# A dilated unfold in one round of matmuls, its outer taps moved by SyncE's DMAs, and the store moved behind the next strip's

## The chip, the cores and the metric

The kernel runs on one core of a Trainium2 chip. The metric is the device time of one execution in microseconds; the median of three runs is given. Engines are named as in the profile: PE multiplies matrices, DVE is the vector engine, ACT the scalar engine, POOL is GpSimd, and SP is SyncE, which here only issues DMAs. Each engine works through its own instructions in order; engines meet at semaphores.

## The reference, cut to what matters

The input `x` is 2 x 128 x 256 x 256, in fp32 throughout. Two residual layers follow each other. Layer 0 normalises in groups, runs a windowed attention with a halo, and adds the result to `x`. Layer 1, the only one that the change touches, is this:

```python
def _L1_conv_ref(x, w1, w3, w4):
    ...
    t1 = jax.lax.conv_general_dilated(x, w1, window_strides=(1, 1), padding=((2, 2), (0, 0)))
    t3 = jax.lax.conv_general_dilated(t1, w3, window_strides=(1, 1), padding=((1, 1), (0, 0)), feature_group_count=c)
    t2 = _unfold_w3_dil2(x)
    t4 = jnp.einsum('nckhw,ckg->nghw', t2, w4[:, :, 0, :])
    t5 = t4[:, None, :, :, :] * t3.reshape(n, c // g, g, h, w)
    return t5.reshape(n, c, h, w)
...
x = x + _L1_conv_ref(_gn(x), L1_conv_w1, L1_conv_w3, L1_conv_w4)
```

`t1` is a vertical convolution of five taps over all 128 channels, and `t3` a vertical convolution of three taps for each channel by itself. `t4` is the horizontal part: `t2` holds, for every pixel, the values two columns to the left, at the pixel, and two columns to the right (zeros outside the image), and `t4` is their product with three 128 x 8 matrices, summed. The eight maps of `t4` are then multiplied into the 128 channels of `t3`, channel c using map c mod 8, and the input of the layer is added.

## The kernel before, in words

The attention layer comes first and writes its result to DRAM strip by strip (`x1_d`). The convolution layer, `convolutions_fast`, then runs over 64 strips: 2 images of 32 strips, 8 image rows each. Channels lie on the 128 partitions. The order of instructions on each engine is the order in which the loop writes them down (`manual_schedule` for all five engines). For strip k the loop does this:

- `load_rows1` (L636, L638) issues on SP the two loads of strip k+2 into one of six `raw` buffers.
- `unfold` (L692) makes `t4`. The 8 rows of the strip are four pairs j; pair j gets the 32 output partitions from 32j on, of which 8 are used. For each of the three taps there are four matmuls, one for each pair, reading the normalised rows `xm` at a column offset of 2 x tap and adding up in one PSUM bank `g`. ACT then copies the bank to `t4` in SBUF (L698).
- `first_rows` copies the two last rows of the strip before on ACT (L723).
- `start_strip` normalises strip k+1: ACT copies four rows that both strips share (L649), DVE normalises the eight new ones from `raw` (L651).
- `vertical(k, 2)` and later `vertical(k, 4)` make four rows of `t1` each, by a scheme that shares products between neighbouring rows: PE makes `a_c` (L706), `a_d` (L740), `a_e` and `a_o` (L706) in a ring of three PSUM banks; ACT copies `a_c` to `both` (L737); DVE makes `c` from `a_d` and `both` (L744) and adds it to `a_e` (L751) and to `a_o` (L757); ACT scales the four rows for the first tap of `t3` (L762).
- `row_sums(k + 1)` makes the next strip's row sums and differences, `sm` (L678 on DVE, one row by ACT, L677) and `df` (L682). It stands between the two halves.
- `depthwise` adds the other two taps of `t3` on DVE (L769, two instructions of 1024 elements per half).
- `spread` (L780) widens `t4` to 128 channels: four matmuls, one for each row pair, with the 0/1 matrix `sel`, of which each uses 32 partitions; the results stand in four banks `b`.
- `combine` (L789) multiplies each bank with its rows of `t3` into `y`, on DVE.
- `finish` (L797, L798) has POOL issue a DMA that adds `x1_d` onto `y`, and SP the store of `y`. SP waits for the first before it issues the second. The last strip is finished in halves with vector additions.

So SP's order is: loads of k+2, store of k, loads of k+3, store of k+1, and so on. `t4`, `t3` and `y` have two buffers each. In strips 1 to 7 some small instructions of the last image's normalisation and of a range test stand between.

Of the kernel before, what the change touches and what calls it, by code (L numbers as in the profile page):

```python
# [9 lines left out]
F32 = mybir.dt.float32  # L10
# [9 lines left out]
P = 128  # L20
W = 256
# [24 lines left out]

def host_constants():
    ident = np.eye(P, dtype=np.float32)  # L50
    gavg = np.zeros((P, P), np.float32)
    for g in range(P // 4):
        gavg[4 * g : 4 * g + 4, 4 * g : 4 * g + 4] = 0.25

    kb = np.zeros((HEADS, 32, 6, 10), np.float32)
    for c in range(10):
        kb[:, c, :, c] = 1.0
    for r in range(6):
        kb[:, 10 + r, r, :] = 1.0
    kb[:, 16, :, 6:] = NEG  # L60
    kb[:, 17, :, :4] = NEG
    flag = np.zeros((2, 4 * NPAIR * 4, 2, 4), np.float32)
    flag[0, :, 0] = 1.0
    flag[1, :, 1] = 1.0


    hot = np.zeros((2, HEADS, 16, 2, 64), np.float32)
    for key in range(64):
        j, i = divmod(key, 6)
        for e in range(2):  # L70
            if 0 <= j - 4 * e < 6:
                hot[:, :, j - 4 * e, e, key] = 1.0
            else:
                hot[:, :, 12, e, key] = NEG
            if key < 60:
                hot[:, :, 6 + i, e, key] = 1.0


    keep = np.zeros((2, HEADS, 16, 2, 2), np.float32)
    for i in range(2):  # L80
        keep[:, i::2, 0:12, i, 0] = 1.0
        keep[:, i::2, 12, i, 1] = 1.0

    sel = np.zeros((4, 32, P), np.float32)
    for ch in range(P):
        sel[:, ch % 8, ch] = 1.0
    return {
        "c_ident": ident,
        "c_sel": sel.reshape(P, P),
        "c_gavg": gavg,  # L90
        "c_kb": kb.reshape(P, 60),
        "c_flag": flag.reshape(2, 4 * NPAIR, 32),
        "c_hot": hot.reshape(P, 128),
        "c_keep": keep.reshape(P, 4),
        "c_head": np.stack([(np.arange(P) // DH % 2 == i) for i in range(2)], 1).astype(np.float32),
    }


class Norms:


    def __init__(self, nc, glob, small, gavg, ns):
        self.nc, self.glob, self.small, self.gavg, self.ns = nc, glob, small, gavg, ns
        self.done = {}
# [478 lines left out]
class Weights:  # L583


    def __init__(self, nc, io, glob):
        self.nc, self.io = nc, io
        self.w1 = glob.tile([P, 5, P], F32, tag="w1", name="w1")
        self.w3 = glob.tile([P, 3], F32, tag="w3", name="w3")
        self.w4 = glob.tile([P, 3, 32], F32, tag="w4", name="w4")  # L590
        self.sel = glob.tile([P, P], F32, tag="sel", name="sel")
        self.w1s = glob.tile([P, 6, P], F32, tag="w1s", name="w1s")

# [13 lines left out]
def convolutions_fast(tc, io, x1_d, norm, st_y, out, weights, count_good):  # L607

    nc = tc.nc
    NB, _, H, _ = io["x"].shape  # L610
    NS = H // 8
    with ExitStack() as l1:
        cst = l1.enter_context(tc.tile_pool(name="f_l1c", bufs=1))
        rawp = l1.enter_context(tc.tile_pool(name="f_raw1", bufs=6))
        tp = l1.enter_context(tc.tile_pool(name="f_t1", bufs=2))
        wk = l1.enter_context(tc.tile_pool(name="f_wk1", bufs=2))
# [4 lines left out]
        w1, w3, w4, sel, w1s = weights.w1, weights.w3, weights.w4, weights.sel, weights.w1s  # L621
# [7 lines left out]
        def load_rows1(b, s):  # L629

            if s == 0:
                pre = rawp.tile([P, 8, W], F32, tag="raw", name=f"raw1_{b}_pre")
                nc.sync.dma_start(pre[:, 5:8, :], x1_d[b][0][:, 0:3, :])
                raws[b, -1] = pre
            t = rawp.tile([P, 8, W], F32, tag="raw", name=f"raw1_{b}_{s}")
            nc.sync.dma_start(t[:, 0:5, :], x1_d[b][s][:, 3:8, :])  # L636
            if s + 1 < NS:
                nc.sync.dma_start(t[:, 5:8, :], x1_d[b][s + 1][:, 0:3, :])  # L638
            raws[b, s] = t
# [15 lines left out]
                nc.gpsimd.memset(cur[:, 4 + n : 12, :], 0.0)  # L655

        t1s, sms, dfs = {}, {}, {}

# [25 lines left out]
        def unfold(k):  # L686

            xt = xn[k % 2]
            pg = ps_pj.tile([P, 512], F32, tag="pj", name=f"g_{k}")
            for tap in range(3):  # L690
                for j in range(4):
                    nc.tensor.matmul(  # L692
                        pg[32 * j : 32 * j + 32, :], w4[:, tap, :],
                        xt[:, 2 * j + 1 : 2 * j + 3, 2 * tap : 2 * tap + W],
                        start=tap == 0, stop=tap == 2,
                    )
            t4 = wk.tile([P, 512], F32, tag="t4", name=f"t4_{k}")
            nc.scalar.copy(t4, pg)  # L698
            t3 = wk.tile([P, 8, W], F32, tag="t3", name=f"t3_{k}")
            y = wk.tile([P, 8, W], F32, tag="y", name=f"y_{k}")  # L700
            ts[k] = t4, t3, y
# [72 lines left out]
        def spread(k):  # L774

            t4 = ts[k][0]
            banks = []
            for j in range(4):
                pb = ps_b.tile([P, 512], F32, tag=f"b{j}", name=f"b_{k}_{j}")
                nc.tensor.matmul(  # L780
                    pb, sel[32 * j : 32 * j + 32, :], t4[32 * j : 32 * j + 32, :], start=True, stop=True
                )
                banks.append(pb)
            return banks
# [9 lines left out]
        def finish(k):  # L794
            b, s = divmod(k, NS)
            t4, t3, y = ts.pop(k)
            nc.gpsimd.dma_start(y, x1_d[b][s], accum_op=ALU.add)  # L797
            nc.sync.dma_start(out[b, :, 8 * s : 8 * s + 8, :], y)  # L798
            del raws[b, s - 1]

        def finish_half(k, half):

            b, s = divmod(k, NS)
            t4, t3, y = ts[k]
            if half == 0:
                nc.gpsimd.tensor_tensor(y[:, 0:3, :], y[:, 0:3, :], raws[b, s - 1][:, 5:8, :], ALU.add)
                nc.gpsimd.tensor_tensor(y[:, 3:4, :], y[:, 3:4, :], raws[b, s][:, 0:1, :], ALU.add)
            else:
                nc.vector.tensor_tensor(y[:, 4:8, :], y[:, 4:8, :], raws[b, s][:, 1:5, :], ALU.add)
            nc.sync.dma_start(  # L810
                out[b, :, 8 * s + 4 * half : 8 * s + 4 * half + 4, :], y[:, 4 * half : 4 * half + 4]
            )

        with tc.manual_schedule(engines=ORDERED):
            for k in range(2):
                load_rows1(*divmod(k, NS))
            start_strip(0)
            row_sums(0)
            for k in range(NB * NS):
                more = k + 1 < NB * NS  # L820
                if k + 2 < NB * NS:
                    load_rows1(*divmod(k + 2, NS))
                unfold(k)
                first_rows(k)
                if more:
                    start_strip(k + 1)

                vertical(k, 2)


                if k in (1, 2):
                    count_good[k - 1](ps_b, "b3")
                if k == 2:
                    steps = norm.steps(st_y[NB - 1], ps_b, f"y{NB - 1}", "b3")
                for _ in range({3: 1, 4: 2, 5: 2, 6: 1, 7: 1}.get(k, 0)):
                    next(steps)
                if more:
                    row_sums(k + 1)
                depthwise(k, 2)
                vertical(k, 4)  # L840
                banks = spread(k)
                combine(k, banks, (0, 1))
                if not more:
                    finish_half(k, 0)
                depthwise(k, 4)
                combine(k, banks, (2, 3))
                if more:
                    finish(k)
                else:
                    finish_half(k, 1)  # L850
# [559 lines left out]
def lay_out(inputs):  # L1410

    c = np.ascontiguousarray
    w_qkv = np.asarray(inputs["L0_conv_W_qkv"])
    rel = np.concatenate(
        [np.asarray(inputs["L0_conv_rel_width"]).T, np.asarray(inputs["L0_conv_rel_height"]).T], axis=1
    )
    w4 = np.asarray(inputs["L1_conv_w4"])[:, :, 0, :]
    return {
        "x": c(np.asarray(inputs["x"])),
        "w_qkvT": c(w_qkv.T),  # L1420
        "w_q": c(w_qkv[:P]),
        "w_outT": c(np.asarray(inputs["L0_conv_W_out"]).T),
        "relT": c(np.tile(rel, (HEADS, 1))),
        "w1T": c(np.asarray(inputs["L1_conv_w1"])[:, :, :, 0].transpose(1, 2, 0)),
        "w3": c(np.asarray(inputs["L1_conv_w3"])[:, 0, :, 0]),
        "w4": c(np.tile(w4, (1, 1, P // w4.shape[-1]))),
        "w4g": c(np.pad(w4, ((0, 0), (0, 0), (0, 32 - w4.shape[-1])))),
        **host_constants(),
    }

# [16 lines left out]
```

## Time and profile before

| what | value |
|---|---|
| median of three runs | 3217.13 us (3214.41 to 3219.65) |
| the profiled execution | 3215.36 us |
| its span | 3213.6 us |
| granted TensorE clock | 0.996 |
| attention, up to the first `unfold` at 2104 us: PE, DVE busy | 1991 us, 1639 us |
| convolutions, 2104 us to the end (1109.6 us): PE, DVE, ACT busy | 1090 us, 972 us, 331 us |

How it is read: all times of the trace are counted from the start of the span, in microseconds, and come from the one profiled execution. "Busy" is the time in which an engine has an instruction under way. A group is written as line, engine, operation, what is written and read, and the shape; `x1408` is the number of records, followed by the busy time in us, the mean ns of one, and the idle time just before its instructions with what ended it. A `SPq` row is the time that SP takes to issue a DMA. The stage of the attention is untouched by the change. The 40 slices show that the convolutions begin after slice 26:

```profile
PE   0799999999999999999999999989999999999998
DVE  8788888888888777777777777679888898888887
DMA  9433333333332222222222222146777676777775
```

### The profile page before, as it was taken

The page shows a single profiled execution, that of the slowest core. Times are in us where ns is not written, and L with a number is a line of the kernel's source. Part 1 is how long each engine was busy: PE and PEld are TensorE (multiplying, and loading weights), DVE is VectorE, ACT ScalarE, POOL GpSimd, SP SyncE. Part 2 cuts the span into 40 slices and gives each one's busy share as a digit, 9 for nine tenths or more (in the row PEclk, how much of TensorE's full clock was granted, in tenths as well). Part 3 has the DMA queues.
Part 4 walks back from the last instruction along what each step waited for, and adds up shares of the span by engine and source line. Part 5 has one row for each costly group of instructions (what it writes and reads, how often), then busy time and mean ns, then how long its engine had stood idle before and what let it go on. Part 6 is the DMA issues. An engine that isn't in the chain of part 4 may idle for free.

```text
span 3213.6 us, 117425 instructions
## 1 busy us (share of the span) xinstructions
PE 3081.7 (96%) x53030; PEld 2280.1 (71%) x53030; DVE 2611.1 (81%) x4152; ACT 1439.9 (45%) x2481; POOL 584.8 (18%) x917
## 2 busy tenths in 40 slices
PE   0799999999999999999999999989999999999998
PEld 0688998899998889999889998844444444444443
DVE  8788888888888777777777777679888898888887
ACT  0455555555555555555555555522332333233322
POOL 2222222222222222222222222100000000000001
PEclk9999999999999999999999999999999999999999
DMA  9433333333332222222222222146777676777775
GB/s 396 149 132 112 122 109 111 108 118 121 111 111 92 85 69 92 81 72 85 69 92 81 72 85 69 56 130 170 190 190 189 180 189 190 184 183 187 193 184 153
DMA packets 125116, 426.42 MB, mean 133 GB/s; under 512 B 9024, under 2 KB 75328, under 8 KB 92096
## 3 DMA queue, kind: packets, MB, share of 16 engines
q1 hardware_dynamic: 115536, 352.76, 32.2%
q0 software_dynamic: 9072, 66.06, 11.3%
q8 instruction: 420, 6.88, 0.9%
q14 instruction: 88, 0.72, 0.1%
HBM read 284.57 MB, written 134.22 MB: 130 GB/s over the span
## 4 chain that ended last, share of the span: by engine, by line
PE 85%; issue 10%; DVE 2%; DMA 1%; POOL 1%; ACT 0%; SPq 0%; POOLq 0%; DVEq 0%; ACTq 0%
PE f_pv L416 15%; PE f_pq L341 8%; PE f_s L451 8%; PE f_o L476 8%; PE a_e L706 7%; PE a_o L706 7%; PE f_pk L341 7%; PE f_py L341 7%; PE f_pa L395 4%; PE f_s L435 4%; PE g L692 4%; PE a_d L740 3%; PE b L780 2%; PE a_c L706 1%; DMA raw<-f_x 1%
## 5 line engine op out<-in xcount | busy, mean ns | idle before, releaser
L422 DVE COPY f_vt<-f_pv 64x512 f32<-64x512 f32 x512 | 354.4, 694 | 292.2 <-ACT f_vt L422 292.0
L416 PE MATMUL f_pv<-f_wqkvT,f_xn 128*128 128x128 f32 x4096 | 491.3, 278 | 0.0
L416 PEld LDWEIGHTS f_pv<-f_wqkvT,f_xn 128*128 128x128 f32 x4096 | 466.9, 192 | 8.6
L762 ACT ACTIVATE t<-t,w 128x1024 f32<-128x1024 f32 x128 | 147.3, 1151 | 687.2 <-DVE t L757 666.8
L323 POOL COPY f_xq<-f_xn 128x256 f32<-128x256 f32 x512 | 310.6, 651 | 756.1 <-DVE f_xn L309 756.1
L376 ACT ACTIVATE f_q<-f_pq,f_head 128x512 f32<-128x512 f32 x512 | 310.2, 688 | 303.4 <-PE f_pq L341 303.4
L460 ACT ACTIVATE f_p<-f_s 128x512 f32<-128x512 f32 x512 | 264.3, 602 | 404.2 <-PE f_s L451 404.2
L422 ACT COPY f_vt<-f_pv 64x512 f32<-64x512 f32 x512 | 297.3, 582 | 118.1 <-PE f_pv L416 117.9
L769 DVE SCALAR_TENSOR_TENSOR t<-t,w,t 128x1024 f32<-128x1024 f32 x256 | 329.9, 1289 | 7.6 <-ACT t L762 1.3
L451 PEld LDWEIGHTS f_s<-f_q,f_kt 64*64 64x64 f32 x16384 | 250.6, 135 | 49.2 <-issue 49.2
L341 PE MATMUL f_pq<-f_xn,f_wq_s 128*128 128x192 f32 (+2 forms) x1520 | 277.1, 329 | 3.3 <-DVE f_xn L309 2.5
L451 PE MATMUL f_s<-f_q,f_kt 64*64 64x64 f32 x16384 | 268.1, 220 | 0.0
L476 PE MATMUL f_o<-f_vt,f_p 128*32 128x66 f32 x16384 | 264.4, 222 | 1.1 <-issue 0.4
L797 POOL DMA_DIRECT2D y<-f_x x63 | 68.1, 1082 | 1017.5 <-DVE y L789 1003.5
L476 PEld LDWEIGHTS f_o<-f_vt,f_p 128*32 128x32 f32 x16384 | 242.5, 110 | 10.6 <-DVE f_cf L408 1.0
L341 PE MATMUL f_pk<-f_xn,f_wqkvT 128*128 128x256 f32 x1024 | 245.2, 380 | 0.0
L341 PEld LDWEIGHTS f_pq<-f_xn,f_wq_s 128*128 128x128 f32 x1520 | 232.4, 188 | 16.9 <-issue 4.2
L341 PE MATMUL f_py<-f_ot,f_woT 128*128 128x256 f32 x1024 | 241.7, 378 | 2.3 <-DVE f_ot L494 2.3
L706 PE MATMUL a_o<-xm,w1s 128*128 128x512 f32 x512 | 240.5, 590 | 0.5 <-ACT both L737 0.5
L706 PE MATMUL a_e<-xm,w1s 128*128 128x512 f32 x512 | 240.7, 591 | 0.0
L300 POOL COPY f_xn<-f_xn 128x1280 f32<-128x1280 f32 x62 | 86.9, 1402 | 772.0 <-PE f_pv L416 772.0
L510 DVE TENSOR_TENSOR f_x<-f_py,f_raw 128x512 f32<-128x512 f32 x256 | 176.0, 688 | 58.1 <-PE f_py L341 50.3
(126 smaller groups left out, 4607.7 us busy)
## 6 DMA issues: line engine op xcount, KB each, us to landing
f_raw<-in_x SPq DMA_DIRECT2D x62, 1280.0 KB, 7.8
f_sx<-in_x SPq DMA_DIRECT2D x64, 1024.0 KB, 7.2
f_x<-f_x SPq DMA_DIRECT2D x128, 512.0 KB, 3.3
y<-f_x POOLq DMA_DIRECT2D x63, 1024.0 KB, 8.2
out<-y SPq DMA_DIRECT2D x63, 1024.0 KB, 4.9
raw<-f_x SPq DMA_DIRECT2D x64, 640.0 KB, 6.4
raw<-f_x SPq DMA_DIRECT2D x62, 384.0 KB, 6.9
f_raw<-in_x SPq DMA_DIRECT2D x2, 1024.0 KB, 7.1
```

Of the source, the lines that this page charges most:

```text
L323: nc.gpsimd.tensor_copy(xq[:, t2, half].rearrange("p t r n c e -> p r t (n c) e"), cells[:, :, 16 * half : 16 * half + 16, 1 + t2 : 9 : 4, ...
L341: nc.tensor.matmul(dst[:, 32 * lo : 32 * hi], w, moving[:, lo:hi], start=True, stop=True)
L376: nc.scalar.activation(q[:, c, :, i], pq.rearrange("p (n x) -> p n x", n=NPAIR), AF.Copy, scale=head[:, i : i + 1],)
L416: nc.tensor.matmul(pv[:, P * n : P * n + P], xn[k % 2][:, r, 4 * j + n].rearrange("p c x -> p (c x)"), wvT, start=True, stop=True,)
L422: (nc.vector.tensor_copy if c else nc.scalar.copy)(vt[rows, 4 * j : 4 * j + 4, :, c, 0:32], pv[rows].rearrange("p (n h d) -> p n h d", n=4 ...
L451: nc.tensor.matmul(sc[g][n // 8][64 * c : 64 * c + 64, n % 8].rearrange("p i x -> p (i x)"), keys_k[rows, c, 48 * n : 48 * n + 64], qs[u][ ...
L460: nc.scalar.activation(pts[u][:, g, 8 * half : 8 * half + 8].rearrange("p n i x -> p (n i x)"), sc[g][half].rearrange("p n i x -> p (n i x ...
L476: nc.tensor.matmul(po[32 * h : 32 * h + 32, n - lo], p[:, h // 2, n, h % 2], vt[:, n, h], start=True, stop=True,)
L510: nc.vector.tensor_tensor(x1[:, :, c:W:2], py.rearrange("p (m t) -> p t m", t=4), raws[k][:, r:8:2, c:W:2], ALU.add,)
L706: nc.tensor.matmul(pa[:, : n * W], w, rows, start=i == 0, stop=i == len(terms) - 1)
L762: nc.scalar.activation(t3[:, j : j + 4], t1[:, j : j + 4, :], AF.Copy, scale=w3[:, 0:1])
L769: nc.vector.scalar_tensor_tensor(t3[:, j : j + 4], t1[:, j + tap : j + tap + 4, :], w3[:, tap : tap + 1], t3[:, j : j + 4], ALU.mult, ALU.add,
```

## The change

Three things change in `convolutions_fast`, with the constants that they need.

1. `unfold` applies all three taps to the same, unshifted pixels at once. The weight of pair j now has the three taps' 8 columns side by side in its 32 columns, in places given by `SLOTS`; four matmuls in one round take the place of twelve in three. The products of the outer taps then belong to a pixel two columns away. ACT copies the bank twice: into `plain`, which has two zero columns on each side, and into `t4`. Five DMAs of SP then overwrite the partitions of the outer taps in `t4` with the same partitions of `plain`, read two columns further left or right. The places are chosen such that neighbouring pairs' outer taps touch, so that five ranges (of 16, 16, 8, 16 and 8 partitions, two rows of 256 values each) are enough.
2. `sel` adds the three taps of a pair up while it spreads them: it has ones at all three places.
3. The store of strip k-1 is no longer issued by `finish`, but in strip k, after `vertical(k, 4)`. SP's order becomes: loads of k+2, five shifts of k, store of k-1, loads of k+3.

```diff
+SLOTS = ((3, 1, 0), (0, 1, 3), (3, 1, 0), (0, 1, 3))
...
-    sel = np.zeros((4, 32, P), np.float32)
-    for ch in range(P):
-        sel[:, ch % 8, ch] = 1.0
+    sel = np.zeros((4, 4, 8, P), np.float32)
+    for j in range(4):
+        for ch in range(P):
+            sel[j, SLOTS[j], ch % 8, ch] = 1.0
...
+        by_pixel = [cst.tile([P, 2, W + 4], F32, tag=f"t4{i}", name=f"t4p_{i}") for i in range(2)]
+        for i in range(2):
+            for side in (0, 2 + W):
+                nc.gpsimd.memset(by_pixel[i][:, :, side : side + 2], 0.0)
...
-            for tap in range(3):
-                for j in range(4):
-                    nc.tensor.matmul(
-                        pg[32 * j : 32 * j + 32, :], w4[:, tap, :],
-                        xt[:, 2 * j + 1 : 2 * j + 3, 2 * tap : 2 * tap + W],
-                        start=tap == 0, stop=tap == 2,
-                    )
-            t4 = wk.tile([P, 512], F32, tag="t4", name=f"t4_{k}")
-            nc.scalar.copy(t4, pg)
+            for j in range(4):
+                nc.tensor.matmul(
+                    pg[32 * j : 32 * j + 32, :], w4[:, j], xt[:, 2 * j + 1 : 2 * j + 3, 2 : 2 + W],
+                    start=True, stop=True,
+                )
+            plain = by_pixel[k % 2]
+            pixels = pg.rearrange("p (r w) -> p r w", w=W)
+            t4 = wk.tile([P, 2, W], F32, tag="t4", name=f"t4_{k}")
+            nc.scalar.copy(plain[:, :, 2 : 2 + W], pixels)
+            nc.scalar.copy(t4, pixels)
+
+            for lo, hi, o in ((24, 40, 0), (88, 104, 0), (0, 8, 4), (56, 72, 4), (120, 128, 4)):
+                nc.sync.dma_start(t4[lo:hi], plain[lo:hi, :, o : o + W])
...
             nc.gpsimd.dma_start(y, x1_d[b][s], accum_op=ALU.add)
-            nc.sync.dma_start(out[b, :, 8 * s : 8 * s + 8, :], y)
+            done[k] = y
             del raws[b, s - 1]
+
+        def store(k):
+            b, s = divmod(k, NS)
+            nc.sync.dma_start(out[b, :, 8 * s : 8 * s + 8, :], done.pop(k))
...
                 vertical(k, 4)
+                if k > 0:
+
+                    store(k - 1)
                 banks = spread(k)
...
+    w4g = np.zeros((P, 4, 4, 8), np.float32)
+    for j in range(4):
+        w4g[:, j, SLOTS[j]] = w4
```

More of the change, by code (lines that the diff above doesn't have):

```diff
@@ L589, in __init__ @@
         self.w3 = glob.tile([P, 3], F32, tag="w3", name="w3")
-        self.w4 = glob.tile([P, 3, 32], F32, tag="w4", name="w4")
+        self.w4 = glob.tile([P, 4, 32], F32, tag="w4", name="w4")
         self.sel = glob.tile([P, P], F32, tag="sel", name="sel")
@@ L657, in convolutions_fast @@
         t1s, sms, dfs = {}, {}, {}
+        done = {}
+        by_pixel = [cst.tile([P, 2, W + 4], F32, tag=f"t4{i}", name=f"t4p_{i}") for i in range(2)]
+        for i in range(2):
+            for side in (0, 2 + W):
+                nc.gpsimd.memset(by_pixel[i][:, :, side : side + 2], 0.0)
         def start_strip(k):
@@ L780, in spread @@
                 nc.tensor.matmul(
-                    pb, sel[32 * j : 32 * j + 32, :], t4[32 * j : 32 * j + 32, :], start=True, stop=True
+                    pb, sel[32 * j : 32 * j + 32, :],
+                    t4[32 * j : 32 * j + 32].rearrange("p r w -> p (r w)"), start=True, stop=True,
                 )
@@ L1426, in lay_out @@
         "w4": c(np.tile(w4, (1, 1, P // w4.shape[-1]))),
-        "w4g": c(np.pad(w4, ((0, 0), (0, 0), (0, 32 - w4.shape[-1])))),
+        "w4g": c(w4g),
         **host_constants(),
```

## The prediction, made before the changed kernel was run

> **What bounds the kernel now.** I read the granted clock first (0.996, so no throttling to explain), then the 40 slices of the page: the change lies in the convolution stage, from 2104 us to the end, where PE and DVE are both near full. So I asked for busy time by stretch inside that stage (columns: window, its length, then busy us and instruction count of PE, weight loads, DVE, ACT, POOL; TensorE clock, DMA share, GB/s).
>
> ```profile
> 2300.00:2840.00 540.00, 539.90 (x2178) 245.62 (x2177) 479.86 (x544) 165.08 (x254) 37.36 (x36) 1.00 0.71 187
> 2870.00:3180.00 310.00, 310.00 (x1241) 141.27 (x1241) 275.21 (x311) 95.31 (x147) 19.54 (x19) 1.00 0.71 185
> ```
>
> PE is busy without a gap, DVE 89%, ACT 31%, the DMA engines 71%. Then the groups by shape from 2200 us on, for the rows that the change touches:
>
> ```profile
> L692 PE MATMUL g<-xm,w 128*32 128x512 f32 x1408 | 163.9, 597 | 0.0
> L780 PE MATMUL b<-t,sel 32*128 32x512 f32 x472 | 67.3, 640 | 0.0
> L698 ACT COPY t<-g 128x512 f32<-128x512 f32 x59 | 34.6, 586 | 62.6 <-PE g L692 62.6
> ```
>
> Each fp32 matmul leaves two records. Next, what DVE waits for over the stage (2111 to 3205 us: total, times, longest):
>
> ```profile
> DVE t L757 <- PE a_o L706: 53.5, 54, 1.9
> DVE df L682 <- ACT sm L677: 27.2, 59, 1.9
> DVE xm L651 <- DMA raw<-f_x: 11.7, 14, 1.5
> DVE t L751 <- PE a_e L706: 2.6, 3, 1.5
> ```
>
> This list is the key one: it says how far DVE is behind PE. Last, the timeline of one strip and the start of the next:
>
> ```profile
> 2707.91 1.14 PE L780 MATMUL b<-t,sel 32*128 32x512 f32 x8
> 2708.98 2.79 PE L692 MATMUL g<-xm,w 128*32 128x512 f32 x24
> 2711.71 0.70 PE L706 MATMUL a_c<-sm,w1s 128*128 128x256 f32 x2
> 2715.08 1.08 POOL L797 DMA_DIRECT2D y<-f_x  x1 [15.42 <-DVE y L789]
> 2718.46 0.69 DVE L757 TENSOR_TENSOR t<-a_o,c 128x512 f32<-128x512 f32 x1 [1.02 <-PE a_o L706]
> 2723.45 0.34 SPq L798 DMA_DIRECT2D out<-y  x1
> 2723.83 0.43 SPq L636 DMA_DIRECT2D raw<-f_x  x1
> 2724.31 0.92 SPq L638 DMA_DIRECT2D raw<-f_x  x1
> 2724.80 1.14 PE L780 MATMUL b<-t,sel 32*128 32x512 f32 x8
> 2725.87 2.78 PE L692 MATMUL g<-xm,w 128*32 128x512 f32 x24
> 2732.75 1.35 DVE L651 TENSOR_SCALAR xm<-raw,mean_y,rstd_y 128x2048 f32<-128x2048 f32 x1 [1.06 <-DMA raw<-f_x]
> ```
>
> A strip takes 2725.87 - 2708.98 = 16.89 us. PE fills it: 2.73 us for g (2708.98 to 2711.71), 13.09 us for the vertical taps (2711.71 to 2724.80), 1.07 us for b. DVE idles 1.02 us at L757 for PE, 0.44 us at L682 for ACT, the rest is short gaps between dependent instructions. So PE sets the pace, with DVE 1.02 us behind it.
>
> **What the Trainium skill says.** "TensorE: Matmul & The Clock Gate", section "Why this matters for your kernels": matmuls with at most 32 output columns in distinct column groups run side by side. The trace agrees: 24 g records take 2.79 us, against six times 0.43 us, the step of untiled 512-column records. "TensorEngine Tiling (Array Packing)", section "Key Properties": a change of tiling mode drains TensorE. The 0.76 us without a weight load ahead of both b and g fits, and their number per strip stays. "DMA: Bandwidth & Descriptors", section "Anatomy of one DMA": about 2.0 us fixed per DMA on GpSimd's path, mostly completion; I use it as the lower bound for a landing. The smallest transfer here (384 KB) lands in 6.9 us, which cannot show it. "Perfetto Trace Analysis", section "Identifying Dependency Chains": an instruction that waits for several engines may get extra semaphore instructions ahead of it; b has none now.
>
> **The change, part by part.**
>
> *Unfolded products (L692).* 12 matmuls in three rounds become 4 in one: 24 records to 8. b, also 8 records four abreast, takes 1.07 us; so g goes from 2.73 to about 1.07 us. PE per strip: 1.07 + 13.09 + 1.07 = 15.23 us, 1.66 less. Bounds 0.93 (2.79 less four steps of 0.43, plus nothing) to 1.14 us; not decisive, as follows.
>
> *What is late next: DVE.* Its work doesn't change. Without the PE wait its strip is 16.89 - 1.02 = 15.87 us, the 0.44 us behind ACT included (L757, then the L762 scaling of 1.15 us and the copy L677 of 0.39 us on ACT, while L678 takes 1.22 us: this stays). The trace has one strip that is paced so: between the second combines at 2187.38 and 2203.47 us DVE never waits for PE, and 16.09 us less some 0.6 us of norm instructions plus 0.3 us of ACT wait then hidden gives 15.8. PE at 15.23 is below it, so of 1.66 us only 1.02 us are collected.
>
> *Does PE keep up with its buffers?* With DVE as pace, PE waits for its three a-banks. In that same strip c of the second half waits for DVE's L744 (starting 2190.58), and from there d, e, o and b end by 2198.73, while DVE's first combine starts at 2199.46: 0.73 us to spare. The first half's o waits for the ACT copy L737 and ended at 2189.76, L757 began at 2191.24: 1.5 us to spare.
>
> *Second ACT copy.* 0.59 us more (row L698; bounds 0.55 to 0.63, the last a strided 512-element copy of L723). Behind it on ACT stand L723, L649 and L737, the last gating o: 1.5 - 0.6 = 0.9 us left. Cost on the path: nothing; without that cover, up to 0.6 us a strip.
>
> *Five shifts on SP.* 64 partitions x 2 rows = 128 pieces of 1 KB, 131 KB. Issue: 0.34 to 0.92 us each by the SPq rows, so 1.7 to 4.6 us. They wait for the ACT copies, which end about 3 us before L651; behind them on SP stand the store of the strip before and the loads of strip k+3. The consumer is b, some 13 us of PE work after g. In the DVE-paced strip the one copy ends at 2185.12, two would by 2185.7, and b starts at 2197.59, 11.9 us later. Landing: unknown; from 2 us (the page) to 8.3 us (an accumulating transfer's 8.2, the slowest load of that strip 8.3). I take 4 us: 2 + 4 = 6, so 6 us early. Even 4.6 + 8.3 = 12.9 would miss by 1.0 us, less 0.73 to spare. Cost taken: 0, high end 0.3 us a strip. Neither end is a gain: a shift adds only waits. DMA share: 0.71 x 16.89 = 12.0 us a strip; 4% more bytes, at most 1.9 us (128 packets at the stage's mean 231 ns, over 16 engines), so 79 to 87% of 15.87.
>
> *Extra waits at b.* Each of the four b matmuls waits for one shift lane or two. Satisfied early, taken at 0; bounded by losing the overlap of the four: 8 x 0.43 - 1.07 = 2.4 us.
>
> *Store moved.* Now SP issues the store (2723.45) when the accumulation lands, 8.4 us after 2715.08, and the loads for two strips on behind it; they land as L651 wants them, hence its 11.7 us of waits. The chain from the end of the combine (2714.79) to L651 (2732.75) is 18.0 us, and from L651 DVE needs 15.87 us to the next combine's end, so it closes over two strips: 2 x period at least 15.87 + 18.0, so 16.9 us. Without the move this chain alone would hold the strip at 16.9. Moved, the loads of k+2 stand behind the store of k-2 instead of k-1: one strip more, 3 x period at least 33.9, 11.3 us. So L651's waits go. Had the store stayed ahead of the shifts, these would wait for the accumulation. The store itself, 8.4 us after its combine, leaves later than the shifts ahead of it; y's two buffers have a strip to spare: 0.
>
> *Smaller weights and padding changes* happen once or outside: 0.
>
> **Sum.** DVE's removable waits: 53.5 + 11.7 + 2.6 = 67.8 us. Staying: 3.4 in the first strip (filling), about 0.7 in strip 32 (three extra 256-column matmuls, 1.4 us, against PE's 0.64 spare), 0.7 in the last strip: 63.0 us go. I deduct 2 us for new small stalls around the norm steps: 61. The profiled execution took 3215.36 us (span 3213.6 and 1.8 around it), 1.8 below the median 3217.13. 3215.4 - 61 = 3154; from the median, 3156.
>
> **Rivals.**
> A. *DVE-paced, as above*: 3156, own range 3148 to 3167.
> B. *DVE-paced with new stalls*: ACT's copy or DMA crowding costs 0.2 to 0.6 us a strip, 13 to 38 us: 3169 to 3194, middle 3181. For: spare of only 0.7 to 0.9 us in two places. Against: in the DVE-paced strip above nothing stalled.
> C. *The loads still bind* (no change): 3217. Needs the three-strip chain to grow from 33.9 to 50 us. Against: 16 us is twice any landing seen.
> D. *Slower: b held on PE.* Waits ahead of b break the four-abreast run, or the shifts land late. PE is in order, so g and the next strip queue behind b. Lost overlap: 15.23 + 2.4 = 17.6 us, 0.74 over today, x 64 = 47: 3264. It decides from 1.66 us of delay a strip on. For: no tiled matmul with a DMA wait is in this trace. Against: the shifts are 6 us early.
>
> **Chances.** A 0.72, B 0.16, C 0.04, D 0.08. A's range misses perhaps a tenth of A; including B's nearer half leaves out about 0.2: 3147 to 3182. The low end is nearly all 67.8 us of waits plus 2 us of measurement spread. About 0.2%, 6 us, can be told from no change: faster 0.88, same 0.04, slower 0.08.
>
> **What would show it.** Right: strips of 15.9 us; g's 8 records in about 1.1 us; L757's wait for PE and L651's for DMA near zero; L682's 0.44 kept; PE now waiting at a_c, a_d, a_e for DVE. Wrong: PE waiting at b for a DMA (D), L744 waiting for ACT's L737 (B), L651 still waiting for raw (C), or DVE instructions that grew longer.

## The result, and where the time went

The changed kernel takes 3144.58 us (median of four runs, 3143.40 to 3146.05), the kernel before, run beside it, 3216.56 us (3214.41 to 3219.65): the ratio is 0.9776, with a 95% interval from 0.9759 to 0.9793. That is 72 us, 2.2%. The forecast was 3156 us with a range from 3147 to 3182 us: the direction and the mechanism hold, the gain is 11 us larger, and the time lies 2.4 us below the range.

In the changed kernel's lines L702 is the unfold, L709 and L710 are the two ACT copies, L713 the shifts, L657 the normalisation, L689 and L693 sums and difference, L759, L766 and L772 are `c` and the two additions, L777 is ACT's scaling, L784 the depthwise taps, L795 b, L805 the combine, L819 the store. First the busy time by stretch inside the convolution stage (columns as before: PE, weight loads, DVE, ACT, POOL, clock, DMA share, GB/s):

```profile
2300.00:2840.00 540.00, 535.22 (x1779) 240.48 (x1778) 510.20 (x581) 188.05 (x304) 38.89 (x38) 1.00 0.78 208
```

DVE rose from 479.86 to 510.20 us of 540, 94%. PE still shows 99%, though it now waits for DVE: the profile's ends of matmuls are modelled and cover short waits, which is why busy PE alone doesn't name the bound. The waits do. DVE's, over 2111 to 3135 us (total, times, longest):

```profile
DVE df L693 <- ACT sm L688: 27.1, 59, 1.9
DVE t L772 <- PE a_o L721: 3.9, 4, 1.9
DVE c L759 <- ACT both L752: 2.2, 1, 2.2
DVE t L766 <- PE a_e L721: 1.5, 1, 1.5
```

The 53.5 us at the addition of `a_o` fell to 3.9, and the 11.7 us for `raw` are gone from the list. The waits of PE's weight loads (`PEld`), from 2300 to 3080 us, show the other side:

```profile
PEld a_c L721 <- DVE t L772: 40.8, 48, 0.9
PEld a_c L721 <- DVE c L759: 39.9, 48, 2.1
...
PEld a_d L755 <- DVE t L766: 24.0, 48, 0.5
```

The first of these is no wait that the change made, though DVE is named in it. The kernel before has the same pause of 0.84 us ahead of the strip's first `a_c`, with no engine to wait for:

```profile
2711.70 0.30 PEld L706 LDWEIGHTS a_c<-sm,w1s 128*128 128x128 f32 x2 [0.84 <-issue]
```

The other two are new: in the second half `a_c` and `a_d` wait until DVE has emptied their banks.

And one strip of the timeline:

```profile
2701.57 1.07 PE L702 MATMUL g<-xm,w 128*32 128x512 f32 x8
...
2702.57 0.70 PE L721 MATMUL a_c<-sm,w1s 128*128 128x256 f32 x2
...
2704.30 3.40 SPq L713 DMA_DIRECT2D t<-t4p  x5
...
2709.31 0.69 DVE L766 TENSOR_TENSOR t<-a_e,c 128x512 f32<-128x512 f32 x1
...
2709.92 0.68 DVE L772 TENSOR_TENSOR t<-a_o,c 128x512 f32<-128x512 f32 x1
...
2715.70 0.34 SPq L819 DMA_DIRECT2D out<-y  x1
...
2716.27 1.14 PE L795 MATMUL b<-t,sel 32*128 32x512 f32 x8
...
2717.34 1.07 PE L702 MATMUL g<-xm,w 128*32 128x512 f32 x8
```

A strip takes 2717.34 - 2701.57 = 15.77 us, against 16.89. Landmarks of DVE in both traces place the difference of the spans, 72.0 us:

| stretch | before | after | gained |
|---|---|---|---|
| start to DVE's statistics near the attention's end | 2097.66 | 2096.79 | 0.87 |
| from there to the second combine of strip 0 | 35.63 | 33.68 | 1.95 |
| from there to the second combine of strip 62 | 1053.74 | 986.29 | 67.45 |
| from there to DVE's last instruction | 19.12 | 17.41 | 1.71 |
| from there to the end | 7.45 | 7.43 | 0.02 |

So 67 of the 72 us lie in the 62 regular strips, 1.09 us each. The theory to be tested: the mechanism is as forecast (PE's round taken away, DVE is next), and the surplus is a price: a listed wait costs more than it is listed with. The rivals: the surplus comes from the moved store (loads that land earlier), or from somewhere else in the shifts and copies.

### The profile page after: what moved, and what is told of

The parts are those of the page before. It is cut to its first block, busy times and chain, and to the rows that moved or that the text cites. A ratio compares the mean times of both kernels' runs of the same rounds, so it can differ in the third digit from the quotient of the medians.

```text
span 3141.6 us, 116082 instructions
## 1 busy us (share of the span) xinstructions
PE 3000.7 (96%) x52006; PEld 2238.9 (71%) x52006; DVE 2604.7 (83%) x4152; ACT 1463.7 (47%) x2545; POOL 583.6 (19%) x921
## 4 chain that ended last, share of the span: by engine, by line
PE 79%; issue 16%; DVE 2%; POOL 2%; DMA 1%; ACT 0%; SPq 0%; POOLq 0%; DVEq 0%
PE f_pv L422 15%; PE f_pq L347 9%; PE f_s L457 8%; PE f_o L482 8%; PE f_pk L347 7%; PE f_py L347 7%; PE a_e L721 5%; PE a_o L721 5%; PE f_pa L401 4%; PE f_s L441 4%; PE a_d L755 2%; PE b L795 1%; PE g L702 1%; POOL y L813 1%; DVE t L766 1%
## 5 line engine op out<-in xcount | busy, mean ns | idle before, releaser
L777 ACT ACTIVATE t<-t,w 128x1024 f32<-128x1024 f32 x128 | 147.1, 1150 | 661.4 <-DVE t L772 642.7
L784 DVE SCALAR_TENSOR_TENSOR t<-t,w,t 128x1024 f32<-128x1024 f32 x256 | 329.9, 1289 | 7.5 <-ACT t L777 1.3
L347 PEld LDWEIGHTS f_pq<-f_xn,f_wq_s 128*128 128x128 f32 x1520 | 232.3, 188 | 16.9 <-issue 4.2
```

The lines of the kernel that those rows point to most:

```text
L347: nc.tensor.matmul(dst[:, 32 * lo : 32 * hi], w, moving[:, lo:hi], start=True, stop=True)
L777: nc.scalar.activation(t3[:, j : j + 4], t1[:, j : j + 4, :], AF.Copy, scale=w3[:, 0:1])
L784: nc.vector.scalar_tensor_tensor(t3[:, j : j + 4], t1[:, j + tap : j + tap + 4, :], w3[:, tap : tap + 1], t3[:, j : j + 4], ALU.mult, ALU.add,
```

## Experiments on the parts of the change

**The store put back, the shifts kept.**

```diff
-            done[k] = y
+            nc.sync.dma_start(out[b, :, 8 * s : 8 * s + 8, :], y)
...
-                if k > 0:
-
-                    store(k - 1)
```

> The changed kernel, with the store of a strip issued by finish again, so that it stands ahead of the next strip's loads and shifts on SP. Theory (the move of the store is needed for the shifts to stay hidden): from the end of a strip's combine to the landed accumulation 8.4 us, two load issues 1.7 us, five shift issues 3.5 us, landing 4 us, so the next b can't start before 17.6 us; b, the combines and the depthwise between them take 6 us more: a strip of about 23 to 24 us against 15.77, so about 3144.6 + 62 x 8 = 3640 us, with PE waiting at b for DMA. Rival (the store's place doesn't matter for the shifts): 3145 us, or 3217 us if only the loads bind.

Measured: 3681.09 us, 1.1439 times the kernel before (1.1417 to 1.1462). The timeline of one strip:

```profile
2714.63 2.42 PE L795 MATMUL b<-t,sel 32*128 32x512 f32 x8 [6.39 <-DMA t<-t4p]
...
2720.64 1.29 DVE L805 TENSOR_TENSOR y<-b,t 128x512 f32<-128x512 f32 x2
...
2722.23 1.08 POOL L813 DMA_DIRECT2D y<-f_x  x1 [23.29 <-DVE y L805]
...
2730.41 0.34 SPq L814 DMA_DIRECT2D out<-y  x1
2730.80 0.42 SPq L642 DMA_DIRECT2D raw<-f_x  x1
2731.27 0.91 SPq L644 DMA_DIRECT2D raw<-f_x  x1
...
2732.29 4.33 SPq L713 DMA_DIRECT2D t<-t4p  x5
...
2739.45 0.80 PEld L795 LDWEIGHTS b<-t,sel 32*128 32x128 f32 x8 [7.91 <-DMA t<-t4p]
```

SP sits at the store until the accumulation, issued at 2722.23, has landed; the shifts stand behind it and b behind them. From 2721.93, the end of the combine, to b it is 17.5 us, as worked out ahead. The rest of the strip is longer than expected, which makes 24.8 us between the starts of b at 2714.63 and 2739.45 instead of 23 to 24: b's eight records took 2.42 and 2.35 us instead of 1.14. The granted clock goes with that. It was 1.00 up to 2711.0, 0.50 from b's start at 2714.63, after a wait of 6.4 us, to 2719.4, and 1.00 again from 2722 us on; over the stretch from 2300 to 2840 us, in which PE works 73% of the time, the mean was 0.85. On this queue the move of the store is not an extra of the change but what keeps the shifts hidden.

**The store moved, nothing else.** The kernel before with `done`, `store(k)` and its call as in the diff of the change, the three rounds kept:

```diff
-            nc.sync.dma_start(out[b, :, 8 * s : 8 * s + 8, :], y)
+            done[k] = y
...
                 vertical(k, 4)
+                if k > 0:
+
+                    store(k - 1)
```

> The kernel before, with only the store moved; the unfold stays in three rounds on PE. Theory (PE sets the pace, and a wait of DVE costs its listed time plus about 0.09 us of overlap that back-to-back instructions would have had): DVE's 11.7 us of listed waits for the raw loads vanish, but PE's 16.89 us a strip stay, and of the strips only the few above 16.95 get shorter: 3211 to 3215 us, with L757's analogue still waiting about 1.02 us for PE in each strip. Rival (the 11 us that the forecast missed come from the store's move): 3205 us or less.

Measured: 3215.97 us, ratio 0.9997 (0.9988 to 1.0005) to the kernel before: no difference, and 1 us above what was expected. DVE's waits over the stage:

```profile
DVE t L758 <- PE a_o L707: 63.9, 62, 1.9
...
DVE xm L651 <- DMA raw<-f_x: 2.8, 1, 2.8
```

The 14 waits for `raw` (11.7 us) are gone. The one that is still listed stands at the stage's very first normalisation, which in the kernel before lay ahead of the window. What the 14 cost comes back at once as waits for PE (63.9 us instead of 53.5). The rival "the surplus comes from the store" falls.

**The shifts left out.**

```diff
-            for lo, hi, o in ((24, 40, 0), (88, 104, 0), (0, 8, 4), (56, 72, 4), (120, 128, 4)):
-                nc.sync.dma_start(t4[lo:hi], plain[lo:hi, :, o : o + W])
```

> The changed kernel without the five shift DMAs: the outer taps' products stay at the wrong columns, everything else is as in the changed kernel. Theory (the shifts are hidden; b is gated by PE and the banks alone): 3144.6 us within 3 us, strips of 15.77 us. Rival (shifts, their issue or the waits at b cost 0.1 to 0.3 us a strip somewhere): 3126 to 3138 us.

Measured: 3144.21 us (3143.62 to 3146.32), 0.4 us from the changed kernel: the five DMAs of a strip, their issue and the waits at b cost nothing that can be seen.

**The loads behind the store, as before.**

```diff
-                if k + 2 < NB * NS:
-                    load_rows1(*divmod(k + 2, NS))
                 unfold(k)
...
                     store(k - 1)
+                if k + 2 < NB * NS:
+                    load_rows1(*divmod(k + 2, NS))
```

> The changed kernel, with the loads of strip k+2 issued on SP behind the store of strip k-1 (after the shifts), as they stood in the kernel before; the shifts stay ahead of the store. Theory (the chain combine, accumulation, store issue, loads, normalise closes over two strips): 2 x period = 15.77 + 18.0, so 16.9 us a strip and about 3144.6 + 62 x 1.1 = 3213 us, with DVE waiting for raw and not for PE. Rival (loads land early enough or faster when PE isn't the pace): 3145 to 3165 us.

Measured: 3193.36 us (3189.67 to 3193.71), 48.8 us slower than the changed kernel. The loads do bind, but less than worked out: 15.77 + 48.8 / 62 = 16.56 us a strip on average, not 16.9. Two strips of the timeline say why:

```profile
2710.73 0.92 SPq L644 DMA_DIRECT2D raw<-f_x  x1
...
2717.18 1.29 DVE L805 TENSOR_TENSOR y<-b,t 128x512 f32<-128x512 f32 x2
...
2718.39 1.34 DVE L657 TENSOR_SCALAR xm<-raw,mean_y,rstd_y 128x2048 f32<-128x2048 f32 x1
2718.76 1.08 POOL L813 DMA_DIRECT2D y<-f_x  x1 [15.94 <-DVE y L805]
...
2726.92 0.34 SPq L819 DMA_DIRECT2D out<-y  x1
...
2727.78 0.93 SPq L644 DMA_DIRECT2D raw<-f_x  x1
...
2736.72 1.35 DVE L657 TENSOR_SCALAR xm<-raw,mean_y,rstd_y 128x2048 f32<-128x2048 f32 x1 [2.48 <-DMA raw<-f_x]
```

From the end of the combine (2718.47) to the normalisation is 18.25 us here; the one at 2718.39, whose combine ended at 2701.67, came 16.7 us after it and didn't wait. Most of the difference lies in the loads: from the issue of the second one to the normalisation it is 8.9 us here (2727.78 to 2736.72) and at most 7.7 us there (2710.73 to 2718.39). So the chain's length changes from strip to strip; the forecast had put the 18.0 us of one strip of the kernel before for all.

## Experiments on the price of a wait

**Three rounds of the new unfold.** PE works as long as before; all else is the changed kernel.

```diff
-            for j in range(4):
-                nc.tensor.matmul(
+            for again in range(3):
+                for j in range(4):
+                    nc.tensor.matmul(
...
```

> The changed kernel, with the round of four unfold matmuls issued three times into the same bank (the last round's result is used, so PE works as long as in the kernel before; shifts, second ACT copy and store order stay). Theory (PE paces again; a wait of DVE that is listed with 1.02 us costs 1.11 us, since the list counts from the reported end of the instruction ahead, and back-to-back independent instructions start some 0.09 us before that end): strips of 15.16 + 2 x 0.86 = 16.88 us, about 3144.6 + 62 x 1.11 = 3213 us, while the listed waits grow by 62 x 1.02 = 63 only. Rival (listed waits are the whole price, the 11 us come from elsewhere in the change): 3208 us or less, strips of 16.79.

Measured: 3215.41 us (3212.85 to 3216.48), 70.8 us over the changed kernel; strips of 16.90 us. DVE's waits over the stage:

```profile
DVE t L773 <- PE a_o L722: 65.2, 62, 1.9
...
DVE c L760 <- ACT both L753: 3.7, 1, 3.7
DVE t L767 <- PE a_e L722: 3.0, 3, 1.5
```

Against the changed kernel the listed waits grow by 61.3 + 1.5 + 1.5 = 64.3 us, the time by 70.8: 6.5 us more. With PE's work given back the whole gain is gone, so shifts, second copy and store order bring none of it by themselves.

**Two rounds.** The same with `range(2)`.

> The same with two rounds. Theory: PE needs 15.16 + 0.86 = 16.02 us a strip, above DVE's 15.77, so strips of 16.02 to 16.05 us and about 3144.6 + 62 x 0.26 = 3161 us; DVE's listed wait for PE is then only 0.17 us a strip, some 10 us in all. Rival (listed waits are the whole price): the listed waits grow by as much as the time, 16 us. A third reading (PE's real floor is above 15.16, and PE and DVE pace together): more than 3165 us.

Measured: 3161.94 us (3161.01 to 3163.05), strips of 16.03 us: 17.4 us more than the changed kernel. The list gives only 15.0 - 3.9 = 11.1 us more at the addition of `a_o`, and 3.4 - 2.2 = 1.2 us more at the first strip's `c`:

```profile
DVE t L773 <- PE a_o L722: 15.0, 55, 1.9
DVE c L760 <- ACT both L753: 3.4, 1, 3.4
```

The timeline shows a single wait:

```profile
2703.49 0.69 DVE L767 TENSOR_TENSOR t<-a_e,c 128x512 f32<-128x512 f32 x1
2704.35 0.69 DVE L773 TENSOR_TENSOR t<-a_o,c 128x512 f32<-128x512 f32 x1 [0.17 <-PE a_o L722]
```

The two start 0.86 us apart; in the changed kernel, without the wait, 0.61 us (2709.31 to 2709.92). The wait costs 0.25 us and is listed with 0.17. So the time exceeds the listed waits by 6.5 us with three rounds and by 17.4 - 12.3 = 5.1 us with two (times are medians of runs that spread over 2 to 4 us, the lists come from one execution each), for 62 and for 55 waits at `a_o`, most of them of about 1.02 and of 0.17 us. That goes with the number of waits, about 0.1 us each, and not with their length: a surplus in proportion to the listed time would have been 1.2 us with two rounds. The dose speaks for the theory, and the PE floor of 15.16 us plus one round of 0.86 gave the strip to 0.01 us.

**ACT's row copy ahead of its scaling.**

```diff
+        def first_sum(k):
+            sms[k] = sm = tp.tile([P, 5, W], F32, tag="sm", name=f"sm_{k}")
+            if k % NS > 0:
+                nc.scalar.copy(sm[:, 0:1], sms[k - 1][:, 4:5])
...
             nc.scalar.copy(both, pa)
+            if m == 2 and k + 1 < NB * NS:
+                first_sum(k + 1)
...
```

> The changed kernel, with ACT's copy of the one shared row of the sums put ahead of its scaling of the first half, right after the copy of a_c, so that DVE's difference no longer waits 0.44 us for ACT. Theory (the wait between sums and difference covers a dependence on DVE itself: in strips where ACT wasn't awaited the difference started 1.32 us after the sums, now 1.65): 0.33 us a strip, about 3144.6 - 60 x 0.33 = 3125 us. Rival (the listed 0.44 us go): 3118 us. Rival (0.44 plus 0.09 of overlap): 3113 us.

Measured: 3125.19 us (3123.82 to 3125.32); strips of 15.43 us. Here the list says too much, 0.44 us for a gain of 15.77 - 15.43 = 0.34:

```profile
2715.94 1.22 DVE L692 TENSOR_TENSOR sm<-xm 128x1024 f32<-128x1024 f32 x1
...
2717.26 1.22 DVE L696 TENSOR_TENSOR df<-sm 128x1024 f32<-128x1024 f32 x1
```

The difference reads what the sums write, so it starts 0.10 us after their reported end even with nothing else to wait for. Whether a wait hides an overlap or a dependence can be read from the same pair of instructions in a strip without the wait.

**The first depthwise tap between sums and difference.**

```diff
...
-                    row_sums(k + 1)
-                depthwise(k, 2)
+                    row_sums(k + 1, lambda: depthwise(k, 2, (1,)))
+                depthwise(k, 2, (2,) if more else (1, 2))
```

> The changed kernel, with DVE's first depthwise tap of the first half placed between the sums and the difference of the next strip. Theory: the ACT wait of 0.44 us, the overlap of 0.09 us and a gap between the two dependent depthwise instructions of about 0.1 us go, so DVE needs 15.1 to 15.2 us, as much as PE's 15.16: strips of 15.2 to 15.3 us, about 3144.6 - 62 x 0.5 = 3113 us. Rival (PE, with three banks to share, can't follow so closely): 3125 us or more.

Measured: 3119.49 us (3119.45 to 3119.73), ratio 0.9695 (0.9679 to 0.9711) to the kernel before, the fastest version of this study; strips of 15.34 us, between the theory's 15.2 to 15.3 and the rival's. PE isn't what holds it, since DVE waits for `a_o` hardly more than in the changed kernel (3.9 us, 4 times):

```profile
DVE t L774 <- PE a_o L723: 4.4, 4, 1.9
```

What seems to hold it is in the timeline:

```profile
2712.76 1.22 DVE L689 TENSOR_TENSOR sm<-xm 128x1024 f32<-128x1024 f32 x1
...
2712.94 1.15 ACT L779 ACTIVATE t<-t,w 128x1024 f32<-128x1024 f32 x1 [4.66 <-DVE t L774]
...
2714.12 1.28 DVE L786 SCALAR_TENSOR_TENSOR t<-t,w,t 128x1024 f32<-128x1024 f32 x1
...
2715.33 1.22 DVE L695 TENSOR_TENSOR df<-sm 128x1024 f32<-128x1024 f32 x1
```

The tap starts 1.36 us after the sums, right after ACT's scaling ends at 2714.09, where an independent neighbour would follow after 1.14 us: the scaling, which the sums used to cover, is 0.2 us too late for it. This is read from the trace and wasn't tried separately.

## What the prediction had right, and the term that failed

- *PE sets the pace, and DVE is next*: right. Putting PE's work back brings 3215 us again, and after the change PE waits at the second half's `a_c` and `a_d` for DVE.
- *PE's new floor*: right within 0.1 us. g's round takes 1.00 us (2701.57 to 2702.57), not 1.07; PE's strip is 15.16 us, not 15.23. The lower bound of 0.93 us for g doesn't come out of its own terms (2.79 - 4 x 0.43 = 1.07), but nothing rests on it.
- *DVE's strip of 15.87 us*: this is the term that failed. It was worked out as 16.89 - 1.02, with the 1.02 us that the list gave for the wait. DVE's strip is 15.77 us, so the wait cost 16.89 - 15.77 = 1.12 us. Before, the additions of `a_e` (the line below) and `a_o` (2718.46) started 1.72 us apart, now 0.61: the idle time is counted from the reported end of the instruction ahead, and an independent neighbour starts 0.08 us before that. The prediction's other estimate, 15.8 from the one DVE-paced strip, was the better one, and was set aside for the list.

```profile
2716.74 0.69 DVE L751 TENSOR_TENSOR t<-a_e,c 128x512 f32<-128x512 f32 x1
```

- *The sum*: for the 62 strips between the landmarks the forecast took 60.8 us (67.8 listed, less 3.4 in the first strip, 2.9 in the last and 0.7 in strip 32) where 67.45 were gained: 6.65 us, for some 70 waits. That is the failed term's share of the 11 us. The deduction of 2 us for new stalls was for nothing: the strips around the norm steps show none. In the first strip the 3.5 us that `c` waited for ACT's `both` had been left out as a start-up cost; 1.3 us of them went, most likely since g stands ahead of `a_c` there too: with three rounds again it is 3.7 us. The remaining 1.5 us of the start differ between the two executions and have nothing of the change in them that could be shown (0.87 us lie in the attention). In the last strip 1.7 us went, where 2.2 had been counted. 6.65 + 2 + 1.3 + 1.5 - 0.5 = 11 us.
- *Second ACT copy at no cost*: right as far as the trace shows; no run leaves it out. It takes 0.57 us, and DVE never waits for `both` in a regular strip.
- *Shifts at no cost*: right, by leaving them out. They land after 4.0 us in the median (2.1 to 6.4), as taken; the DMA share is 0.78, just under the range given.
- *The store's place*: right in kind. Ahead of the shifts it costs 536.5 us. That the loads alone would hold the strip at 16.9 us without the move was too much: 16.56.
- *Extra waits at b*: right. From 2300 to 3080 us each b of the changed kernel has one more semaphore instruction ahead of it, of 51 ns, and its eight records still take 1.14 us.
- *Rivals B, C and D*: none came. The range's low end had been set at all listed waits plus 2 us, on the reading that nothing beyond the list could go; that reading was the mistake.

The landing of the shifts, over 2300 to 3080 us of the changed kernel (issue time on SP in ns, minimum, median and maximum, then the time to landing):

```profile
L713 SPq DMA_DIRECT2D t<-t4p x245: 587/613/1524, 2307.7 to 3069.8; - x123
...
DMA to landing us min/median/max: 2.1/4.0/6.4
```

## What to carry to other kernels

Work out the pace of the next engine from the starts of its instructions in a stretch where it doesn't wait, not by taking listed idle time off the present pace. On DVE the two differed here by about 0.1 us for each wait: the end of a wait between independent instructions gained that much more than was listed, the end of one between dependent instructions that much less. When a DMA is moved onto a queue, look at what that queue waits for ahead of it; here the order of three kinds of DMAs on SP decides between 3145, 3193 and 3681 us. A wait that a change removes may only have been cover for a wait for another engine, as the moved store alone showed.

## What the runs showed of the hardware that was not expected

- In these traces a DVE instruction that doesn't read its predecessor's output started 0.08 us before the predecessor's reported end (L766 and L772 of the changed kernel); one that does started about 0.10 us after it (L692 and L696 with the early row copy).
- With the store put back PE waited 6.4 us for the shifts. When it went on, the granted clock was 0.50 for some 5 us (2714.63 to 2719.4) before it was 1.00 again, and eight four-abreast records took 2.42 us instead of 1.14.
- A shift of 16 or 32 KB from SBUF to SBUF occupied SP for 0.6 us in the median, between the 0.43 and 0.92 us of the loads of 640 and 384 KB, and took 4.0 us to land beside the other transfers.
